# Layer 0 by seven block products, fewer PSUM banks for the sums, and a VectorE transpose for the row of scores

## The chip, the core and the metric

The kernel runs on one core of a Trainium2 chip. A core has five engines with a queue each: TensorE (PE) multiplies matrices into PSUM, VectorE (DVE) and ScalarE (ACT) do elementwise work, GpSimd (POOL) a few small operations, SyncE (SP) issues DMAs. Each queue is worked off in order, and engines wait for one another by semaphores. The metric is the device time of one launch in microseconds (us), the median of several runs.

## The reference

32 graphs, each with 512 nodes of 256 features and a 0/1 adjacency matrix, go through four attention layers. Every layer normalises the features, takes relu, and adds what the layer gives to x. Cut to what matters:

```python
h = maximum(layernorm(x), 0)
# layer 0: attention by a bilinear score, two rounds of convolution
q = h @ att_W;  score = q @ h.T / sqrt(256)
p = softmax(score + where(adj == 1, 0, -1000))
y = tanh(p @ (h @ W0 + b0));  x = x + tanh(p @ (y @ W1 + b1))
# layers 1, 2: score of an edge = a number of its row + a number of its column
Wh = h @ W.T                       # layer 2: h @ W
e = leaky_relu((Wh @ a1)[:, None] + (Wh @ a2)[None, :])
x = x + softmax(where(adj > 0, e, -9e15)) @ Wh       # layer 2: exp(-e), masked, divided by its row sum, elu
# layer 3: both kinds of score together, then two projections
f = h @ W;  logits = (f @ a_1).T + f @ a_2 + (f @ a_12) @ f.T
x = x + elu(h @ W_1 + (softmax(masked leaky_relu(logits)) @ h) @ W_2)
```

All products are in float32.

## The kernel before

A graph is worked in tiles of 128 nodes (NT = 4) and 128 features (HC = 2). `normed` computes the statistics on VectorE, a power on GpSimd, the scaled relu on ScalarE, then splits the float32 numbers into two 16-bit planes (VectorE), turns each by a DMA transpose, and joins them again (ScalarE, L488). The result is hT, features on partitions.

`attend` (L662) multiplies the transposed weights of the attention, tile by tile, by the values v, which carry a column of ones for the row sums. Layer 0 uses the same weights a second time (`again`, L723), and projects with W1 (L741).

Every step is recorded with `op(engine, cost, after, emit, ...)`: its engine, an assumed time (how long it holds the engine, and until when its result is there), the steps it waits for, and the buffers that it uses. `Plan.order` then puts the steps of all 32 graphs in an order, engine by engine, by these times and by a rank for each graph; at most FLIGHT = 5 graphs are under way. The instructions are emitted in this one order, and the framework adds the semaphore waits. So the order of each queue is fixed when the program is built, and can be read from it. Buffers of 4 KB a partition come from a pool of 36 pages; PSUM has 8 banks.

**Seven block products.** In layer 3 a product of two matrices, each cut into 2 x 2 blocks, is made from seven products of blocks in place of eight. `block_sums` forms four sums of blocks of a factor on VectorE (L570), `seven_of` does it once for a weight matrix, and `seven` runs the products:

```python
first = times(1, 0, True)                       # times(product, bank, fresh)
c11 = out(write, 0, 0, 0, first)
c12 = out(write, 0, 1, 0, times(6, 0, False, c11))
c22 = out(write, 1, 1, 0, times(7, 0, False, c12))
c21 = out(write, 1, 0, 0, times(4, 0, False, c22))
c11 = out(add, 0, 0, 1, times(2, 1, True, first), c11)
c22 = out(add, 1, 1, 2, times(5, 2, True, first), c22)
c12 = out(add, 0, 1, 2, times(3, 2, False, c22), c12)
```

Products 1, 6, 7, 4 add up in bank 0, which is written out after each; product 2 is in bank 1, products 5 and 3 in bank 2, and these are added to what was written. It is used for the features (L838, written by ScalarE L841, added by VectorE L846), the values (L855, L865, L868), the scores (L878, written by VectorE L885, added by L893) and the projection w (L855, L946, L950) of layer 3.

**Layer 0 without it.** `features_t` makes fa with att_sb (L513, copied by ScalarE L517), the values come from L682 (bias added by VectorE L686), the scores from L696, whose exponential ScalarE takes straight from PSUM (L700); VectorE applies the mask (L703).

**Row of scores in layers 1 and 2.** `scored_values` multiplies hT by weights with two more columns (L596); these give each node two numbers, which VectorE copies to `sd` (L600): the number of node 128 t + p lies at partition p, place t. `leaky_exp_t` needs the first number of all nodes as a row on every partition. In the first five and last five graphs TensorE turns it (L619); in the 22 others a DMA writes it to DRAM and a second one spreads it over the partitions (L624, L628), with the nodes in the order p, t. ScalarE then reads it with a step of 4 elements and applies the leaky relu (L635), and the exponential (L639).

**Weights.** ScalarE's queue issues the loads of w0, att and b0 first (L363 to L365), GpSimd's queue those of the other weights; the preparation of layers 1 to 3 runs on TensorE and VectorE beside graph 0.

Of the kernel before, what the change touches and what calls it, by code (L numbers as in the profile page):

```python
# [11 lines left out]
F32 = mybir.dt.float32  # L12
# [7 lines left out]
P = 128  # L20
# [22 lines left out]
V_SUM, V_INTO, V_BLOCK = (334.0, 425.0), (640.0, 730.0), (790.0, 880.0)  # L43
# [3 lines left out]
D_OUT, D_SPREAD = (550.0, 3500.0), (550.0, 4500.0)  # L47
# [111 lines left out]
def kernel(  # L159
# [37 lines left out]
    PAGES, VALUES = 36, 4  # L197
# [20 lines left out]
        "st": ([P, NT, 6], F32, None), "mv": ([P, NT, 2], F32, None), "sd": ([P, 2, NT], F32, None),  # L218
# [3 lines left out]
    POOLS = {"page": PAGES, "v": VALUES, "code": 1, "adj": 1, "planes": 3, "planesT": 2, "bank": 8,  # L222
# [129 lines left out]
    att_sb, w0_sb, w1_sb = (tile_of(n, H) for n in ("att_sb", "w0_sb", "w1_sb"))  # L352

    l3_w1s, m3 = (tile_of(n, HALF, 7) for n in ("l3_w1s", "m3"))
# [8 lines left out]
    nc.scalar.dma_start(out=w0_sb, in_=rows_of(w0))  # L363
    nc.scalar.dma_start(out=att_sb, in_=rows_of(att_w))
    nc.scalar.dma_start(out=b0_sb, in_=line_of(b0))  # L365
    ready["w1"] = [load(w1_sb, rows_of(w1))]
# [32 lines left out]
    for i in range(VALUES):  # L399
        v = const.tile([P, NT, LEAD + H + 1], F32, tag=f"v{i}", name=f"v{i}")  # L400
        nc.gpsimd.memset(v[:, :, LEAD + H :], 1.0)
        v_bufs.append(v)


    def graph(b, adj_before, x_before):
# [99 lines left out]
        def features_t(l, hs, w_sb, ready):  # L505

            done = []
            for k in range(HC):
                key = f"bank_f{l}{k}"

                def product(k, key):
                    for c in range(HC):
                        nc.tensor.matmul(T[key], w_sb[:, c, k * P : (k + 1) * P], T[f"hT{l}"][:, c, :],  # L513
                                         start=(c == 0), stop=(c == HC - 1))

                def evacuate(k, key):
                    nc.scalar.copy(T[f"fa{l}"][:, k, :], T[key])  # L517

                a = op("PE", pe(n512=4), hs + ready, partial(product, k, key), key, f"hT{l}")
                done.append(op("A", A_COPY, [a], partial(evacuate, k, key), key, f"fa{l}"))  # L520
            return done

        def seven(key, cost, after, keys, work, write, add):

            def times(x, k, fresh, *wait):
                name = f"bank_{key}{k}"
                return op("PE", cost, after(x) + list(wait), lambda: work(x, T[name], fresh), name, *keys)

            def out(how, i, l, k, *wait):
                return how(i, l, f"bank_{key}{k}", list(wait))


            first = times(1, 0, True)
            c11 = out(write, 0, 0, 0, first)
            c12 = out(write, 0, 1, 0, times(6, 0, False, c11))
            c22 = out(write, 1, 1, 0, times(7, 0, False, c12))
            c21 = out(write, 1, 0, 0, times(4, 0, False, c22))
            c11 = out(add, 0, 0, 1, times(2, 1, True, first), c11)  # L550
            c22 = out(add, 1, 1, 2, times(5, 2, True, first), c22)
            c12 = out(add, 0, 1, 2, times(3, 2, False, c22), c12)
            return {(0, 0): c11, (0, 1): c12, (1, 0): c21, (1, 1): c22}
# [31 lines left out]

        def scored_values(l, hs, w_aug, ready):
# [4 lines left out]
            for t in range(NT):  # L591
# [7 lines left out]
                def scores(t, key):  # L599
                    nc.vector.tensor_copy(T[f"sd{l}"][:, : cols - H, t], T[key][:, H:cols])  # L600
# [9 lines left out]
        def leaky_exp_t(l, ss, sign):  # L610

            turned = b < FLIGHT or b >= B - FLIGHT
# [3 lines left out]
            def turn(t):  # L618
                nc.tensor.transpose(T[key][:, t * P : (t + 1) * P],  # L619
                                    T[f"sd{l}"][:, 0, t : t + 1].to_broadcast([P, P]), ident)  # L620

            def collect():
                line.append(dram.tile([P, NT], F32, tag=f"row_{T.places['slot']['number']}", name=f"row{l}_{b}"))
                nc.sync.dma_start(out=line[0], in_=T[f"sd{l}"][:, 0, :])  # L624
# [5 lines left out]
            def leaky(c):  # L630
                if turned:
                    row = T[key].rearrange("q (t p) -> q t p", t=NT)
                else:
                    row = T[key][:, 0, :].rearrange("q (p t) -> q t p", t=NT)
                nc.scalar.activation(e(l, c).rearrange("q (t p) -> q t p", t=NT), row, AF.Prelu,  # L635
                                     bias=T[f"sd{l}"][:, 1, c : c + 1], alpha=ALPHA)
# [8 lines left out]
            else:  # L645
                a = op("D", D_OUT, ss, collect)
                a = op("D", D_SPREAD, [a], spread, key)
            ls = [op("A", A_PRELU, [a], partial(leaky, c), key, f"e{l}_{c // 2}") for c in range(NT)]
# [22 lines left out]

        hs = normed(0, [got_x] * NT)
        qs = features_t(0, hs, att_sb, [])
        vs = []
        for g in range(NT // 2):
            key = f"bank_v0{g}"

            def values(g, key):
                for j in range(2):
                    t = 2 * g + j  # L680
                    for c in range(HC):
                        nc.tensor.matmul(T[key][:, j * H : (j + 1) * H], T["hT0"][:, c, t * P : (t + 1) * P],  # L682
                                         w0_sb[:, c, :], start=(c == 0), stop=(c == HC - 1))

            def biased_v(g, j, key):
                nc.vector.tensor_add(T["v0"][:, 2 * g + j, LEAD : LEAD + H], T[key][:, j * H : (j + 1) * H], b0_sb)  # L686

            a = op("PE", pe(n256=8), hs[two(g)], partial(values, g, key), key, "hT0")
            vs += [op("V", V_ADD, [a], partial(biased_v, g, j, key), key, "v0") for j in range(2)]
        es = []  # L690
        for c in range(NT):
            key = f"bank_q{c}"

            def similar(c, key):
                for k in range(HC):
                    nc.tensor.matmul(T[key], T["hT0"][:, k, c * P : (c + 1) * P], T["fa0"][:, k, :],  # L696
                                     start=(k == 0), stop=(k == HC - 1))

            def exp0(c, key):
                nc.scalar.activation(e(0, c), T[key], AF.Exp, scale=float(H) ** -0.5)  # L700

            def masked0(c):
                nc.vector.tensor_tensor(e(0, c), e(0, c), T["mask0"][:, c, :], ALU.mult)  # L703

            a = op("PE", pe(n512=4), qs, partial(similar, c, key), key, "hT0", "fa0")
            a = op("A", A_COPY, [a], partial(exp0, c, key), key, f"e0_{c // 2}")
            es.append(op("V", V_MASK, [a, m0], partial(masked0, c), "mask0", f"e0_{c // 2}"))
# [128 lines left out]

# [21 lines left out]
        def two_tiles(key, k):  # L858
            return T[key][:, : 2 * k].rearrange("p (j k) -> p j k", j=2)
# [172 lines left out]
```

The softmax here doesn't subtract the row's maximum and nothing guards it: scores larger than these inputs give would overflow.

## Time and profile before

| | |
|---|---|
| median of 3 runs | 2461.58 us (2461.34 to 2461.85) |
| the profiled execution | 2461.46 us, its span from first to last instruction 2459.7 us |
| granted TensorE clock | 0.998 |
| TensorE matmul busy | 2407.4 us, 10700 records |
| TensorE weight loads busy | 1877.3 us |
| VectorE busy | 1876.2 us |
| ScalarE busy | 1742.8 us |
| time between the same step of two graphs in the middle | 75.3 us |

The profile is of one execution. Records of an engine can overlap: the end of one lies behind the start of the next, so the busy time of a row divided by its count is shorter than the mean duration where instructions follow each other closely. A float32 product appears as two matmul records. In rows of groups the columns are: line, engine, operation, output and inputs, shapes, count; then busy us and mean ns of one; then the idle time in front of it and what ended it. In rows of waits they are: who waited for whom, us in total, times, and the longest.

### The profile page before, as it was taken

Reading aid. Unit: us, or ns where it says so; the run is one execution under the profiler, and the core shown is the slowest. Engines: PE = TensorE matmul, PEld = TensorE weight load, DVE = VectorE, ACT = ScalarE, POOL = GpSimd, SP = SyncE. Lnnn points to the kernel's source line nnn. Section 1 sums busy time; section 2 is a strip of 40 time slices with the busy share of each in tenths; the row PEclk is TensorE's granted clock in tenths of the full one; section 3 lists DMA queues with packets and bytes.
Section 4 is the critical chain, followed back from the end, with each engine's and each line's share of the span. In section 5 each row is a group of like instructions: output and inputs, shape, how many; then the busy total and the mean of one; then the engine's idle time right before and its main releaser. Section 6 shows DMA issues by size and latency. Waiting matters only on the chain.

```text
span 2459.7 us, 33966 instructions
## 1 busy us (share of the span) xinstructions
PE 2407.4 (98%) x10700; PEld 1877.3 (76%) x10700; DVE 1876.2 (76%) x5733; ACT 1742.8 (71%) x3233; POOL 253.8 (10%) x315
## 2 busy tenths in 40 slices
PE   7999999999999999999999999999999999999998
PEld 4678777777777777777777777777777777777877
DVE  5468878777777877787777777777777778756888
ACT  4466777767777777777677777777776777755884
POOL 2001001110010101011101101010011011100110
PEclk9999999999999999999999999999999999999999
DMA  7223333332333322333323333233333343321221
GB/s 178 46 56 82 73 69 82 82 74 54 80 76 82 82 64 64 80 80 82 71 54 81 74 82 82 64 65 80 80 76 70 62 83 81 71 46 22 44 46 41
DMA packets 437204, 175.92 MB, mean 72 GB/s; under 512 B 393408, under 2 KB 410432, under 8 KB 437024
## 3 DMA queue, kind: packets, MB, share of 16 engines
q1 hardware_dynamic: 430976, 154.34, 29.9%
q0 software_dynamic: 5360, 18.75, 2.3%
q8 instruction: 85, 1.39, 0.2%
q14 instruction: 95, 0.78, 0.1%
q10 hardware_dynamic: 688, 0.66, 0.1%
HBM read 64.49 MB, written 16.87 MB: 33 GB/s over the span
## 4 chain that ended last, share of the span: by engine, by line
PE 73%; ACT 17%; DVE 5%; issue 3%; DMA 2%; POOL 0%; SPq 0%; POOLq 0%; ACTq 0%; DVEq 0%
PE bank_a L662 28%; PE bank_v L596 9%; PE bank_z L723 9%; ACT e L635 8%; PE bank_o L741 4%; PE bank_f L513 4%; PE bank_f L838 4%; PE bank_w L855 4%; ACT e L639 3%; PE bank_q L696 3%; PE bank_v L855 3%; PE bank_s L878 3%; ACT xn L475 2%; PE bank_v L682 2%; ACT e L700 1%
## 5 line engine op out<-in xcount | busy, mean ns | idle before, releaser
L662 PE MATMUL bank_a<-v,e 128*128 128x257 f32 (+1 forms) x4096 | 978.0, 381 | 21.8 <-ACT y L714 17.5
L662 PEld LDWEIGHTS bank_a<-v,e 128*128 128x128 f32 x4096 | 757.9, 190 | 199.9 <-issue 68.6
L488 ACT COPY hT<-planesT 128x512 uint16<-128x512 uint16 x512 | 383.2, 767 | 42.1 <-DMA planesT<-planes 41.7
L468 POOL TENSOR_TENSOR rstd<-ve,mhalf 128x2 f32<-128x2 f32 x256 | 215.2, 849 | 1891.7 <-DVE ve L465 1807.6
L475 ACT ACTIVATE xn<-x,off,rstd 128x256 f32<-128x256 f32 x512 | 277.3, 593 | 123.1 <-DVE off L471 119.3
L596 PE MATMUL bank_v<-l_aug,hT 128*128 128x258 f32 x1024 | 251.5, 383 | 3.3 <-ACT r L807 1.7
L480 DVE COPY planes<-xn 128x512 uint16<-128x512 uint16 x512 | 207.9, 422 | 43.8 <-ACT xn L475 24.1
L723 PE MATMUL bank_z<-e,y 128*128 128x512 f32 x512 | 240.6, 592 | 0.0
L696 PE MATMUL bank_q<-fa,hT 128*128 128x512 f32 x512 | 239.3, 592 | 0.0
L596 PEld LDWEIGHTS bank_v<-l_aug,hT 128*128 128x128 f32 x1024 | 192.2, 191 | 35.5 <-issue 3.6
L461 DVE BATCH_NORM_STATS2 st<-x 128x6 f32<-128x256 f32 x512 | 209.0, 408 | 6.6 <-DMA x<-in_x_dram 6.6
L635 ACT ACTIVATE e<-row,sd 128x512 f32<-128x512 f32 x176 | 207.0, 1229 | 0.0
L603 ACT COPY v<-bank_v 128x256 f32<-128x256 f32 x256 | 92.9, 375 | 90.1 <-PE bank_v L596 75.8
L639 ACT ACTIVATE e<-e 128x512 f32<-128x512 f32 x256 | 151.9, 632 | 0.0
L696 PEld LDWEIGHTS bank_q<-fa,hT 128*128 128x128 f32 x512 | 94.9, 190 | 71.4 <-issue 60.8
L723 PEld LDWEIGHTS bank_z<-e,y 128*128 128x128 f32 x512 | 96.5, 190 | 69.1 <-issue 57.9
L885 DVE SCALAR_TENSOR_TENSOR e<-bank_s,v,mask 128x256 f32<-128x256 f32 x256 | 111.1, 476 | 16.5 <-PE bank_s L878 16.3
L682 PE MATMUL bank_v<-w_sb,hT 128*128 128x256 f32 x512 | 121.4, 380 | 0.0
L703 DVE TENSOR_TENSOR e<-e,mask 128x512 f32<-128x512 f32 x128 | 87.5, 688 | 44.0 <-ACT e L700 43.9
L741 PE MATMUL bank_o<-w_sb,zT 128*128 128x256 f32 x512 | 120.4, 379 | 0.0
L513 PE MATMUL bank_f<-hT,att_sb 128*128 128x512 f32 x256 | 119.8, 593 | 0.0
L682 PEld LDWEIGHTS bank_v<-w_sb,hT 128*128 128x128 f32 x512 | 97.1, 191 | 23.9 <-issue 6.1
(134 smaller groups left out, 3702.1 us busy)
## 6 DMA issues: line engine op xcount, KB each, us to landing
adj<-in_adj_dram SPq DMA_DIRECT2D x128, 256.0 KB, 2.9
x<-in_x_dram SPq DMA_DIRECT2D x32, 512.0 KB, 5.1
out_dram<-y POOLq DMA_DIRECT2D x32, 512.0 KB, 4.1
row<-row SPq DMA_DIRECT2D x44, 256.0 KB, 3.7
planesT<-planes SPq DMA_TRANSPOSE x512, 2.4
codeT<-code SPq DMA_TRANSPOSE x128, 2.6
crest<-crest SPq DMA_TRANSPOSE x64, 2.4
raw_w<-in_L_gnn_W_dram POOLq DMA_DIRECT2D x3, 256.0 KB, 7.1
```

The lines of the kernel that those rows point to most:

```text
L468: nc.gpsimd.tensor_tensor(T[f"rstd{l}"][:, two(g)], T[f"ve{l}"][:, two(g)], mhalf[:, two(g)], ALU.pow)
L475: nc.scalar.activation(T[f"xn{l}"][:, t, :], T["x"][:, t, :], AF.Relu, bias=T[f"off{l}"][:, t : t + 1], scale=T[f"rstd{l}"][:, t : t + 1])
L488: nc.scalar.copy(bits[:, :, :, t * P : (t + 1) * P], T[f"planesT{l}_{t}"].rearrange("p (b c) n -> p b c n", b=2))
L513: nc.tensor.matmul(T[key], w_sb[:, c, k * P : (k + 1) * P], T[f"hT{l}"][:, c, :], start=(c == 0), stop=(c == HC - 1))
L596: nc.tensor.matmul(T[key][:, :cols], T[f"hT{l}"][:, c, t * P : (t + 1) * P], w_aug[:, c, :], start=(c == 0), stop=(c == HC - 1))
L635: nc.scalar.activation(e(l, c).rearrange("q (t p) -> q t p", t=NT), row, AF.Prelu, bias=T[f"sd{l}"][:, 1, c : c + 1], alpha=ALPHA)
L639: nc.scalar.activation(e(l, c), e(l, c), AF.Exp, scale=sign)
L662: nc.tensor.matmul(T[keys[j]][:, : LEAD + H + 1 - lead], e(l, c)[:, t * P : (t + 1) * P], T[f"v{l}"][:, c, lead:], start=(c == 0), stop=(c ...
L682: nc.tensor.matmul(T[key][:, j * H : (j + 1) * H], T["hT0"][:, c, t * P : (t + 1) * P], w0_sb[:, c, :], start=(c == 0), stop=(c == HC - 1))
L696: nc.tensor.matmul(T[key], T["hT0"][:, k, c * P : (c + 1) * P], T["fa0"][:, k, :], start=(k == 0), stop=(k == HC - 1))
L723: nc.tensor.matmul(T[f"bank_z{k}"], T["y0"][:, c, k * P : (k + 1) * P], e(0, c), start=(c == 0), stop=(c == NT - 1))
L741: nc.tensor.matmul(T[key][:, j * H : (j + 1) * H], T["zT"][:, k, t * P : (t + 1) * P], w1_sb[:, k, :], start=(k == 0), stop=(k == HC - 1))
```

## The change

It has four parts.

1. Layer 0's features, values and scores are made by `seven` as well. att and w0 are loaded into pages and cut into seven block matrices by VectorE (`seven_of`); sums hs0 of hT and fs0 of fa are formed for every graph. The values are written and added by VectorE, the features written by ScalarE and added by VectorE. Of the scores, three blocks are copied by ScalarE, get their addition from VectorE and then their exponential in SBUF; the fourth gets its exponential from PSUM.
2. `seven` holds one or two banks in place of three: products 2, 5 and 3 go to bank q, or (`beside`) to the second half of bank p. Features (layers 0 and 3), layer 0's values and w are of the second kind. Products 2 and 5 wait for more than before.
3. The two numbers of each node go to a buffer that is kept for a graph's slot and starts at zero: tile t's first number to column 32 t, its second to column 128 + t. In the middle graphs a VectorE transpose of 32 x 32 squares puts the first numbers on partitions 0, 32, 64 and 96; the DMA from there writes them in the order of the nodes, and the leaky relu reads a contiguous row.
4. Pages 35 for 36, and other assumed times for some steps.

```diff
-V_SUM, V_INTO, V_BLOCK = (334.0, 425.0), (640.0, 730.0), (790.0, 880.0)
+V_SUM, V_BLOCK = (334.0, 425.0), (790.0, 880.0)
+V_SQUARES = (180.0, 270.0)
-D_OUT, D_SPREAD = (550.0, 3500.0), (550.0, 4500.0)
+D_OUT, D_SPREAD = (550.0, 2500.0), (550.0, 4500.0)
...
-    nc.scalar.dma_start(out=w0_sb, in_=rows_of(w0))
-    nc.scalar.dma_start(out=att_sb, in_=rows_of(att_w))
+    w0_sb, att_sb = raw("raw9"), raw("raw10")
     nc.scalar.dma_start(out=b0_sb, in_=line_of(b0))
+    for n, dst, w, key in (("att", att_s, att_w, "raw10"), ("w0", w0_s, w0, "raw9")):
+        a = prepare("A", (500.0, 4000.0), [], lambda w=w, key=key: nc.scalar.dma_start(out=raw(key)(), in_=rows_of(w)), key)
+        ready[n] = seven_of(raw(key), dst, HALF, [a], key)
...
+    score_bufs = []
+    for i in range(FLIGHT):
+        s = const.tile([P, P + NT], F32, tag=f"scores{i}", name=f"scores{i}")
+        nc.gpsimd.memset(s, 0.0)
+        score_bufs.append(s)
...
+        def seven(key, cost, after, keys, work, write, add, beside=0):
+            p, q = f"bank_{key}p", f"bank_{key}{'p' if beside else 'q'}"
+            def times(x, bank, start, fresh, *wait):
+                return op("PE", cost, after(x) + list(wait), lambda: work(x, T[bank][:, start:], fresh), bank, *keys)
+            c11 = write(0, 0, p, 0, [times(1, p, 0, True)])
+            two = times(2, q, beside, not beside, c11)
+            c12 = write(0, 1, p, 0, [times(6, p, 0, False, c11)])
+            c22 = write(1, 1, p, 0, [times(7, p, 0, False, c12)])
+            four = times(4, p, 0, False, c22)
+            c21 = write(1, 0, p, 0, [four])
+            c11 = add(0, 0, q, beside, [two, c11])
+            c22 = add(1, 1, q, beside, [times(5, q, beside, True, four, c11), c22])
+            c12 = add(0, 1, q, beside, [times(3, q, beside, False, c22), c12])
...
-                    nc.vector.tensor_copy(T[f"sd{l}"][:, : cols - H, t], T[key][:, H:cols])
+                    nc.vector.tensor_copy(scores_of()[:, 32 * t : P + 1 + t : P - 31 * t], T[key][:, H:cols])
...
+            def squares():
+                nc.vector.transpose(T[f"sT{l}"], scores_of()[:, :P])
...
-                nc.sync.dma_start(out=line[0], in_=T[f"sd{l}"][:, 0, :])
+                nc.sync.dma_start(out=line[0].rearrange("(t g j) -> g t j", t=NT, j=32),
+                                  in_=T[f"sT{l}"][0:P:32, :].rearrange("g (t j) -> g t j", t=NT))
...
-                nc.scalar.activation(e(l, c).rearrange("q (t p) -> q t p", t=NT), row, AF.Prelu,
-                                     bias=T[f"sd{l}"][:, 1, c : c + 1], alpha=ALPHA)
+                row = T[key] if turned else T[key][:, 0, :]
+                nc.scalar.activation(e(l, c), row, AF.Prelu, bias=scores_of()[:, P + c : P + c + 1], alpha=ALPHA)
...
+        right_after, right = block_sums("hs0", "hT0", lambda j, l, T=T: T["hT0"][:, j, half(l)], hs, left=False)
+        qs = features_t(0, right_after, right, att_s, ready["att"])
...
+        vs = seven("v0", pe(nt=4), lambda x, after=right_after: after(x) + ready["w0"], ("hT0", "hs0"),
+                   partial(by_nodes, w0_s, right), write_v0, add_v0, beside=N // 2)
+        left_after, left = block_sums("fs0", "fa0", lambda i, j: T["fa0"][:, j, half(i)], qs, left=True)
...
+        def write_q(i, l, key, start, after):
+            if (i, l) == (1, 0):
+                return op("A", A_COPY, after, partial(exp0, i, l, key), key, f"e0_{l}")
+            return op("A", A_COPY, after, lambda: nc.scalar.copy(block_e0(i, l), two_tiles(key, 0, N // 2)), key, f"e0_{l}")
+        def add_q(i, l, key, start, after):
+            a = op("V", V_MASK, after, lambda: nc.vector.tensor_tensor(
+                block_e0(i, l), block_e0(i, l), two_tiles(key, 0, N // 2), ALU.add), key, f"e0_{l}")
+            exps.append(op("A", A_EXP, [a], partial(exp0, i, l), f"e0_{l}"))
+            return exps[-1]
...
+        qb = seven("q0", pe(n256=4), lambda x, right_after=right_after, left_after=left_after: right_after(x) + left_after(x),
+                   ("hT0", "hs0", "fa0", "fs0"), partial(scores0, right, left), write_q, add_q)
+        es = {il: op("V", V_MASK, [a, m0], partial(masked0, *il), "mask0", f"e0_{il[1]}") for il, a in qb.items()}
```

## The prediction

> **What bounds the kernel now.** I read the busy times first, then the stretches in which nothing starts or ends, then what TensorE waits for there, and last the groups of the lines that the change touches.
>
> ```profile
> PE 2407.4 (98%) x10700; PEld 1877.3 (76%) x10700; DVE 1876.2 (76%) x5733; ACT 1742.8 (71%) x3233; POOL 253.8 (10%) x315
> ...
> PE   7999999999999999999999999999999999999998
> ```
>
> TensorE is busy in every slice but the first and last. "Busy" can flatter it, since its records overlap, so I took the stretches, and 18 whole graphs (607.87 to 1963.95 us, 75.34 us each):
>
> ```profile
> 0.00:20.00 20.00, 4.98 (x22) 4.53 (x22) 8.25 (x33) 3.46 (x5) 12.26 (x30) 1.00 0.98 278
> ...
> 607.87:1963.95 1356.08, 1340.14 (x5941) 1045.58 (x5941) 1052.05 (x3205) 1000.84 (x1819) 139.03 (x162) 1.00 0.34 74
> ```
>
> The columns are length, then busy PE, PEld, DVE, ACT, POOL, then granted clock. In the middle PE lacks 0.89 us a graph; VectorE is busy 58.4 us and ScalarE 55.6 us of 75.34. Over the whole span PE is idle 52 us: about 16 in the first 40 us, 16 in the last 160, the rest in the middle. There the waits name one cause, once a graph:
>
> ```profile
> PE bank_a L662 <- ACT y L714: 15.7, 18, 0.9
> ```
>
> So the middle is bound by TensorE's stream, and what is saved there comes off the time if PE stays fed. The pace of the stream is read from starts, not from durations (each has 0.16 us of tail that overlaps):
>
> ```profile
> 1050.28 0.60 PE L855 MATMUL bank_w<-l_w1s,hT 128*128 128x128 f32 x4
> 1050.72 1.04 PE L662 MATMUL bank_a<-v,e 128*128 128x259 f32 x4
> ...
> 1000.74 1.88 PE L696 MATMUL bank_q<-fa,hT 128*128 128x512 f32 x4
> 1002.46 0.61 PE L855 MATMUL bank_v<-l_aug,hT 128*128 128x129 f32 x4
> ```
>
> Four records of 128 columns take 0.44 us (110 ns each), four of 512 columns 1.72 us (429 ns). An f32 product is two such records. Over the 18 graphs the mean from start to start is 111, 215.5 and 429 ns for 128, 256 and 512 columns.
>
> **The products of layer 0.** Features: 8 records of 512 (8 x 0.429 = 3.43 us) become 14 of 256 (3.02), -0.42. Values: 16 of 256 (3.45) become 28 of 128 (3.11), -0.34. Scores: 16 of 512 (6.86) become 28 of 256 (6.03), -0.83. Together -1.60 us a graph, x32 = **-51 us**, if the short records flow as now.
>
> A rule speaks against the values' part. The Trainium skill (TensorE: Matmul & The Clock Gate, "LDWEIGHTS (loading the stationary operand)") makes a weight load cost its columns over 1.2 GHz, 107 ns for 128 columns whatever the products behind it. Then a 128-column record is as short as its load, and if the two alternated, each would cost about 217 ns: 28 x 0.217 = 6.1 us in place of 3.45, +84 us over all graphs. The rows above show 110 ns with a new load before each record, so load and stream overlap; I use 111.
>
> **What VectorE gets.** Its rows are costed from start to start as well: a pair of L686 (0.42 us each) fills 0.75 us, so each holds VectorE 0.33.
>
> ```profile
> 1014.17 0.75 DVE L686 TENSOR_TENSOR v<-bank_v,b_sb 128x256 f32<-128x256 f32 x2
> ...
> L893 DVE TENSOR_TENSOR e<-e,bank_s 128x512 f32<-128x512 f32 x96 | 64.7, 681 | 3.0 <-PE bank_s L878 2.9
> ```
>
> Per graph: 8 block sums (hs0, fs0) x 0.33 = 2.7; 3 additions of features 1.0; values 7 in place of 4, +1.0; 3 additions of scores like L893, 0.60 each, 1.8; the masks stay 4. In the 22 graphs that spread by DMA, two 128x128 transposes: no row of before is one; the nearest, a 128x128 VectorE copy at the start, took 0.22 us, and 0.31 is the price in the Trainium skill (VectorE: DVE Perf Modes, "The three transpose paths", for bf16). I take 0.25, ends 0.2 and 0.6: 0.5 a graph. Sum +7.0: VectorE comes to 65.4 of some 74 us, **88%** instead of 78%. It is no bound, but it is now close enough that its queue answers late.
>
> **What ScalarE gets.** Features 4 copies at 0.32 for 2 at 0.53, +0.2; scores 3 copies and 3 more exponentials in place of 3, +1.7. Against that the row of scores lies in order, so L635 no longer reads every fourth element:
>
> ```profile
> L635 ACT ACTIVATE e<-row,sd 128x512 f32<-128x512 f32 x176 | 207.0, 1229 | 0.0
> ...
> L635 ACT ACTIVATE e<-bank_r,sd 128x512 f32<-128x512 f32 x80 | 52.4, 693 | 14.0 <-PE bank_r L619 13.9
> ```
>
> The contiguous form costs 0.69 to 0.72 (L924 reads SBUF, 716 ns): 8 x -0.52 = -4.2 us a graph in the middle. ScalarE ends at about 53 us a graph. I give this **0 us** of the time: ScalarE is off the path, five graphs overlap, and the work that hides it is TensorE's stream. If that cover were gone it would be worth 4 us a graph. The DMA pair behind it is hidden too (SP issues the same two DMAs a layer; the first now carries 16 runs of 128 B in place of 128 of 16 B); SP's queue gets nothing new.
>
> **What the banks cost.** This is the part that the trace of before cannot show. In layer 3 the first write chain had a bank of its own and the additions two others; ScalarE and VectorE never read the same bank. Now features of layers 0 and 3 and the w product hold all in one bank, written by ScalarE, added by VectorE. The Trainium skill (PSUM — Partial Sum Buffer, "PSUM bank collisions raise a hardware error") says that any two engines on one bank must be kept apart, readers too, at whatever columns. The built program's queues do so: in graph 16, the VectorE addition of product 2 stands behind product 4, ScalarE's write of product 4 waits for that addition, and product 5 waits for ScalarE. Counting from the start of product 4: result 0.60 (two records of 256, as L838), addition 0.42 (L846), copy 0.38 (L603), three hops of 0.05: 1.55 us. Between the two TensorE has product 4 itself (0.43) and one pair of 129-column products (0.44). It stands for **0.68 us**. By the rows alone, columns being disjoint, it would be nothing; by the program's waits I take them. Going so through the queues of graphs 16 and 17, I find one or two such places each, 0.5 to 0.7 us a graph; in the same stretch of before none. I take 0.5 x 32 = **+16 us**. Ends: 0 (VectorE and ScalarE ahead, other work in between) and 2 us a graph, +64 (all three chains catching).
>
> **The old stall.** L662 waiting for L714 is a wait for a bank to come free. Fewer banks are held now, and behind the tanh the new queue has 2.6 us of other products. But VectorE at 88% will be late elsewhere. From -0.87 x 22 = -19 to +30; I take **-6 us**.
>
> **The start.** Before, VectorE's first work is graph 0's statistics at 5.64 us; the weights of layer 0 are used as they land.
>
> ```profile
> 5.64 0.43 DVE L461 BATCH_NORM_STATS2 st<-x 128x6 f32<-128x256 f32 x1 [4.77 <-DMA x<-in_x_dram]
> ...
> 12.69 0.15 DVE L471 SCALAR_TENSOR_TENSOR off<-mv,rstd 128x2 f32<-128x2 f32 x1
> ```
>
> Now the seven block matrices of att and w0 stand ahead of those statistics in VectorE's queue, and ScalarE's queue issues b0, att, w0 in that order. Its last of the same 640 KB landed at 11.4 us (issue at 1.83, 9.6 to landing). Then 1.4 us of blocks, 2.2 of statistics, and power, code and copies as before: the offset of L471 comes at about 17.3, 4.6 later, and 16 us behind it TensorE's first features. Part is slack (TensorE did preparation from 26.3 to 28.9). The first f and q chains are also serial, where no other graph fills. I take **+6 us**, ends +2 and +12. **The end:** layer 3's additions come after product 4 now, about 1 us for each of its chains, partly filled by the second last graph: **+2**, ends 0 and 5.
>
> **Sum.** -51 + 16 - 6 + 6 + 2 = -33. The profiled execution took 2461.46 us (span 2459.7 and 1.8 around it), 0.1 under the median of 2461.58; so **2428 us**.
>
> **Rivals.**
> - The stream saving comes whole (0.18): the short distances are filled, because VectorE and ScalarE run ahead. -51 - 14 + 6 = 2402. For it: PE lacked only 0.89 us a graph so far. Against: VectorE's 10% more.
> - The banks eat most of it (0.17): all mixed chains catch, 1 to 1.5 us a graph, -51 + 32 to 48: 2443 to 2458. For it: the waits are in the program; against: in most places the queue has over 0.8 us between.
> - **Slower (0.07):** VectorE becomes the bound. It is an in-order queue, and each addition that now waits for a later product holds all behind it: block sums, masks and statistics of other graphs. It decides once these holds exceed 75.3 - 65.4 = 9.9 us a graph; twelve mixed-bank reads a graph at 0.9 us would do it. At 11 us a graph the period is 76.4, +35, with the start +6: about 2500; right at the point, 2468.
> - That the change does not do what it says is left out for the products: the queues hold 5876 products for 5396, 32768 columns fewer, as counted above.
>
> **How the numbers follow.** My case (2412 to 2443) 0.58, full saving 0.18, banks 0.17 (a quarter of that within 0.2% of before), slower 0.07 (2 of it within). 0.2%, 4.9 us, is about what a measurement of this kernel can tell from no change: 2456.7 to 2466.5. Faster 0.89, same 0.05, slower 0.06. The range leaves out the ends: 2402 to 2454.
>
> **What would show it.** Right: PE's stretch per middle graph near 73 us of stream; L855-like 128-column records of bank_v0 at 111 ns; waits of PE on bank_f, released by ACT fa, of 0.3 to 0.7 us once or twice a graph; VectorE 86 to 90% busy; the first features after 30 us; L635's successor near 0.7 us. Wrong: PE waits of over 2 us a graph, or VectorE busy over 95% in the middle (then slower); PE idle under 0.5 us a graph (then 2402); 128-column records at over 150 ns.

## The result, and the profile after

| | before | after |
|---|---|---|
| median | 2461.46 us (2460.83 to 2461.85, 4 runs) | 2425.9 us (2423.93 to 2429.52, 4 runs) |
| ratio to before on the same chip | | 0.9857, 95% interval 0.984 to 0.9875 |
| profiled execution, its span | 2461.46, 2459.7 us | 2423.93, 2422.2 us |
| one graph in the middle (output of graph to output of graph, mean of 18) | 75.32 us | 73.46 us |

The forecast of 2428 us was 2 us off. The experiments below show that errors cancel in this sum; how large they are depends on the order in which the parts are counted (see the last sums of the section on the prediction). First the page of after, its rows of busy time and TensorE's slices:

```profile
PE 2372.1 (98%) x11660; PEld 1988.7 (82%) x11660; DVE 2059.8 (85%) x6333; ACT 1727.2 (71%) x3393; POOL 252.0 (10%) x320
...
PE   6999999999999999999999999999999999999998
```

TensorE has 960 records more and 35.3 us less of busy time. VectorE rose by 184 us, ScalarE fell by 16. The same stretches as before, from the busy times of windows (length, then PE, PEld, DVE, ACT, POOL, clock):

```profile
0.00:20.00 20.00, 4.40 (x20) 4.02 (x20) 7.04 (x31) 1.67 (x2) 10.36 (x31) 1.00 0.66 201
...
607.87:1963.95 1356.08, 1350.21 (x6673) 1139.33 (x6672) 1183.96 (x3648) 1000.11 (x1961) 138.62 (x167) 1.00 0.35 77
```

VectorE is busy 87% of this stretch, where 88% was forecast. The short records flow as computed. From the timeline of PE (start, duration; four records are two products):

```profile
856.20 0.61 PE L702 MATMUL bank_v0p<-w_s,hs 128*128 128x128 f32 x4
856.64 1.03 PE L906 MATMUL bank_s3p<-hs,fa 128*128 128x256 f32 x4
857.51 1.03 PE L729 MATMUL bank_q0p<-fa,hs 128*128 128x256 f32 x4
```

From 856.20 to 856.64 four records of 128 columns pass, 110 ns each, each behind a new weight load. The Trainium skill (TensorE: Matmul & The Clock Gate, "LDWEIGHTS (loading the stationary operand)") has 107 ns for a load of 128 columns; the load records here last 191 ns, and still the products follow each other every 110 ns. Loads and products do not alternate, and the doubled price was rightly left out. The load records of layer 0's values, and the groups of the row of scores:

```profile
L702 PEld LDWEIGHTS bank_v0p<-w_s,hs 128*128 128x128 f32 x512 | 73.7, 191 | 7.9 <-DVE v L714 2.1
...
L632 ACT ACTIVATE e<-row,scores 128x512 f32<-128x512 f32 x176 | 117.6, 711 | 0.0
...
L619 DVE STREAM_TRANSPOSE sT<-scores 128x128 f32<-128x128 f32 x44 | 13.5, 306 | 0.3
```

The leaky relu takes 711 ns where it took 1229, and the transpose of squares 306. Of TensorE's waits, those of before for a bank that ScalarE's tanh holds (L714 there) are gone; in the middle this is left:

```profile
PE bank_f0p L676 <- ACT fa L684: 4.3, 9, 0.5
PE bank_v3p L702 <- ACT v L893: 0.3, 1, 0.3
```

This is the wait that the prediction worked out from the queues. One of them in the timeline of after:

```profile
839.77 0.59 PE L676 MATMUL bank_f0p<-hs,att_s 128*128 128x256 f32 x2
840.20 0.61 PE L702 MATMUL bank_v3p<-l_aug,hT 128*128 128x129 f32 x4
840.40 0.42 DVE L691 TENSOR_TENSOR fa<-fa,bank_f0p 128x256 f32<-128x256 f32 x1 [0.67 <-PE bank_f0p L676]
...
840.86 0.37 ACT L684 COPY fa<-bank_f0p 128x256 f32<-128x256 f32 x1 [0.85 <-DVE fa L691]
...
841.28 0.70 PE L676 MATMUL bank_f0p<-hs,att_s 128*128 128x256 f32 x2 [0.47 <-ACT fa L684]
```

Product 4 starts at 839.77, VectorE adds at 840.40, ScalarE copies at 840.86, product 5 starts at 841.28: 1.51 us, 1.55 were computed. TensorE had work until 840.20 + 4 x 0.11 = 840.64, so it stood 0.64 us (0.68 computed). The row says 0.47, because the last record before it ends 0.17 us after its place in the stream (840.81 for 840.64). A stall shorter than that tail shows as no idle time at all. Therefore I measure a **gap** from here on as the time from the start of a matmul record to the next start, less the pace of its shape (111, 217 or 429 ns), where that leaves over 25 ns. Stretches of a few us in which the profile's granted clock is halved are left out of the sums. Sums of such gaps in the profiled executions, split at the fifth and the 23rd output to leave:

| gaps, us | to the 5th output | 5th to 23rd | from there on | sum |
|---|---|---|---|---|
| before | 8.2 | 21.0, all L662 | 15.3 | 44.5 |
| after | 23.2 | 14.8, 12.7 of it bank_f0p | 14.2 | 52.2 |

After has more gaps than before. So of the 51 us of stream that the change saves, and the wait for the tanh that went, much was given back, and the question is which part of the change brought what.

### The profile page after: what moved, and what is told of

It reads as the page before. It is cut to its first block, busy times and chain, and to the rows that moved or that the text cites. A ratio compares the mean times of both kernels' runs of the same rounds, so it can differ in the third digit from the quotient of the medians.

```text
span 2422.2 us, 36547 instructions
## 1 busy us (share of the span) xinstructions
PE 2372.1 (98%) x11660; PEld 1988.7 (82%) x11660; DVE 2059.8 (85%) x6333; ACT 1727.2 (71%) x3393; POOL 252.0 (10%) x320
## 3 DMA queue, kind: packets, MB, share of 16 engines
q8 instruction: 92, 1.51, 0.3%
## 4 chain that ended last, share of the span: by engine, by line
PE 88%; ACT 4%; DVE 3%; issue 3%; DMA 1%; POOL 0%; ACTq 0%; POOLq 0%; DVEq 0%
PE bank_a L659 34%; PE bank_z L774 9%; PE bank_v L591 8%; PE bank_o L792 4%; PE bank_q0p L729 4%; PE bank_s3p L906 4%; PE bank_f0p L676 4%; PE bank_v0p L702 4%; PE bank_w3p L702 3%; PE bank_f3p L676 3%; PE bank_q0q L729 3%; PE bank_s3q L906 3%; PE bank_v3p L702 2%; PE bank_v3q L702 2%; ACT xn L484 1%
## 5 line engine op out<-in xcount | busy, mean ns | idle before, releaser
L659 PE MATMUL bank_a<-v,e 128*128 128x257 f32 (+1 forms) x4096 | 976.1, 381 | 7.9 <-ACT e L632 2.7
L659 PEld LDWEIGHTS bank_a<-v,e 128*128 128x128 f32 x4096 | 757.7, 190 | 158.9 <-issue 49.6
L635 ACT ACTIVATE e<-e 128x512 f32<-128x512 f32 x256 | 153.1, 626 | 0.0
L632 ACT ACTIVATE e<-row,scores 128x512 f32<-128x512 f32 x176 | 117.6, 711 | 0.0
L913 DVE SCALAR_TENSOR_TENSOR e<-bank_s3p,v,mask 128x256 f32<-128x256 f32 x256 | 111.2, 476 | 6.9 <-PE bank_s3p L906 6.8
L686 ACT ACTIVATE fa<-bank_f3p,l_u 128x256 f32<-128x256 f32 x128 | 60.6, 473 | 74.3 <-PE bank_f3p L676 71.9
L471 DVE BATCH_NORM_AGGREGATE mv<-st 128x2 f32<-128x6 f32 x512 | 93.2, 182 | 17.5
L792 PEld LDWEIGHTS bank_o<-w_sb,zT 128*128 128x128 f32 x512 | 96.4, 190 | 13.9 <-DVE st L470 0.2
L737 ACT ACTIVATE e<-e 128x512 f32<-128x512 f32 x96 | 60.6, 631 | 50.7 <-DVE e L746 50.0
L800 ACT ACTIVATE z<-z 128x512 f32<-128x512 f32 x64 | 40.2, 629 | 74.3 <-DVE z L796 74.2
```

The source lines that it names most:

```text
L659: nc.tensor.matmul(T[keys[j]][:, : LEAD + H + 1 - lead], e(l, c)[:, t * P : (t + 1) * P], T[f"v{l}"][:, c, lead:], start=(c == 0), stop=(c ...
L792: nc.tensor.matmul(T[key][:, j * H : (j + 1) * H], T["zT"][:, k, t * P : (t + 1) * P], w1_sb[:, k, :], start=(k == 0), stop=(k == HC - 1))
```

## Experiments

Times are medians of four runs; the ratio is to the kernel before on the same chip, which took 2463.3 to 2465.6 us beside these. Its 95% interval reaches some 0.15% to either side. "Period" is the time of a graph in the middle as above.

### The row of scores alone

The kernel before with part 3 of the change, and products, banks and weights as before:

```diff
+                nc.vector.transpose(T[f"sT{l}"], scores_of()[:, :P])
...
-                    row = T[key][:, 0, :].rearrange("q (p t) -> q t p", t=NT)
+                row = T[key] if turned else T[key][:, 0, :]
```

> The kernel before with the new way of the row of scores alone (VectorE transpose, ordered DMA, contiguous read by ScalarE); layer 0 by eight products, three banks a chain. Theory: ScalarE loses 90 us of work that was hidden; within 8 us of before, 2454 to 2462. Rival: in the old order ScalarE held banks (the wait of L662 for the tanh, 0.87 us a graph), and its relief takes that wait away: 2435 to 2450 us.

2439.1 us (2438.64 to 2439.43), ratio 0.9892 [0.9877, 0.9907], period 74.24. The part that I had costed at nothing brings 0.0108 x 2462 = 27 us when it is made alone, as much as three quarters of the whole gain. The waits of L662 for the tanh are gone, and gaps of TensorE fall from 44.5 to 18.0 us. This kernel has a new order of all queues, so the next one keeps the old order.

### ScalarE's read alone, in the order of before

```diff
-                    row = T[key][:, 0, :].rearrange("q (p t) -> q t p", t=NT)
+                    row = T[key][:, 0, :].rearrange("q (t p) -> q t p", t=NT)
```

> The kernel before in its own queue order and with its own DMAs; only ScalarE's leaky relu of the 22 middle graphs reads the row contiguously (the row is then permuted, so that part of the result differs). Theory (the tanh came late because the strided read holds ScalarE 0.5 us longer than the order assumes, 8 times a graph): ScalarE busy falls by 80 to 95 us, the wait of L662 for the tanh (15.7 us in the 18 middle graphs) falls below 3 us, period 74.2 to 74.6 for 75.32, time 2436 to 2446. Rival (row_only's gain came from its new order and shorter DMA times in the plan): the wait stays over 10 us, period 75.1 or more, time 2455 to 2466.

2439.99 us (2436.99 to 2442.23), ratio 0.9902 [0.9887, 0.9917], period 74.15. The theory holds: queues and DMAs are as before (the scores only reach the nodes in another order), and nothing but the duration of one ScalarE instruction has changed,

```profile
L635 ACT ACTIVATE e<-row,sd 128x512 f32<-128x512 f32 x176 | 116.8, 714 | 0.0
```

and the gaps of the middle go from 21.0 to 0.0 us. TensorE is busy without a break there:

```profile
607.87:1963.95 1356.08, 1356.08 (x6048) 1065.76 (x6047) 1078.10 (x3257) 952.65 (x1854) 134.26 (x165) 1.00 0.35 76
```

How a ScalarE at 71% came to hold TensorE is in the timeline of before, ahead of one of the waits (lines of DVE, ACT and TensorE's L662):

```profile
789.73 1.20 ACT L635 ACTIVATE e<-row,sd 128x512 f32<-128x512 f32 x1
790.79 6.66 PE L662 MATMUL bank_a<-v,e 128*128 128x257 f32 x30
790.84 0.61 ACT L639 ACTIVATE e<-e 128x512 f32<-128x512 f32 x1
...
791.49 0.69 DVE L764 TENSOR_TENSOR e<-e,mask 128x512 f32<-128x512 f32 x1 [1.25 <-ACT e L639]
...
795.88 0.69 DVE L902 TENSOR_TENSOR crest<-e 128x512 bf16<-128x512 f32 x1
...
796.60 1.33 ACT L924 ACTIVATE e<-e,zero 128x512 f32<-128x512 f32 x2 [0.47 <-DVE crest L902]
...
797.84 0.82 ACT L714 ACTIVATE y<-bank_a,rs 128x256 f32<-128x256 f32 x2
798.34 0.92 PE L662 MATMUL bank_a<-v,e 128*128 128x257 f32 x3 [0.89 <-ACT y L714]
```

The mask L764 waits 1.25 us for an exponential behind a strided L635. All of VectorE's queue is then late, L902 with it; ScalarE's L924 waits for L902, and the tanh that frees a PSUM bank stands behind L924 in ScalarE's queue. The lateness is handed from ScalarE to VectorE and back before it reaches TensorE. With the contiguous read the same L764 waits 0.22 us, the same tanh follows its reciprocal at once, and the products run on:

```profile
787.29 0.69 DVE L764 TENSOR_TENSOR e<-e,mask 128x512 f32<-128x512 f32 x1 [0.22 <-ACT e L639]
...
790.82 6.45 PE L662 MATMUL bank_a<-v,e 128*128 128x257 f32 x29
...
793.83 0.91 ACT L714 ACTIVATE y<-bank_a,rs 128x256 f32<-128x256 f32 x2
```

Of VectorE's waits in the middle of before, these show the first hop (us, times, longest):

```profile
DVE e L703 <- ACT e L700: 27.2, 19, 1.7
DVE e L764 <- ACT e L639: 23.4, 19, 1.6
DVE e L791 <- ACT e L639: 23.1, 18, 1.9
```

With the contiguous read these three are 10.0, 1.8 and 0.9 us, and VectorE's three largest waits in the middle are for TensorE:

```profile
DVE rs L711 <- PE bank_a L662: 45.1, 70, 1.6
DVE rs L799 <- PE bank_a L662: 33.6, 33, 1.7
DVE rs L774 <- PE bank_a L662: 23.4, 55, 1.3
```

### The strided read, its duration told to the order

Before assumes 0.57 us for the leaky relu (0.69 to its result), in all graphs. Was the wrong figure in the order the fault, or the longer work itself?

```diff
+A_STEP = (1115.0, 1229.0)
...
-            ls = [op("A", A_PRELU, [a], partial(leaky, c), key, f"e{l}_{c // 2}") for c in range(NT)]
+            ls = [op("A", A_PRELU if turned else A_STEP, [a], partial(leaky, c), key, f"e{l}_{c // 2}") for c in range(NT)]
```

> The kernel before with the strided read kept, and its real duration (1.12 held, 1.23 to result) in the order's assumptions for the middle graphs, for 0.57 and 0.69. Theory (an order made with a wrong duration, not lack of ScalarE): the new order has the tanh in time, the wait of L662 falls below 5 us in the middle, period 74.2 to 74.8, time 2436 to 2450. Rival (ScalarE's longer work itself costs it, wherever it stands): the wait or its like stays over 10 us, 2453 to 2468.

2453.42 us (2450.35 to 2454.84), ratio 0.9955 [0.9941, 0.997], period 74.73. The time, and a wait of over 10 us, are those of the rival; only the period lies in the theory's range. The tanh is in time, but another result of ScalarE is late in its place, the joined hT.

```profile
PE bank_v L597 <- ACT hT L489: 10.4, 10, 2.3
```

So this order regains about 11 us of the 24 to 27. Whether another one would regain more is not shown.

### The strided read in the changed kernel

After in its own order of queues, with the old access in the 22 middle graphs:

```diff
-                row = T[key] if turned else T[key][:, 0, :]
+                row, to = (T[key], e(l, c)) if turned else (T[key][:, 0, :].rearrange("q (p t) -> q t p", t=NT),
+                                                            e(l, c).rearrange("q (t p) -> q t p", t=NT))
```

> The changed kernel with every queue in the same order; only ScalarE's leaky relu in the 22 middle graphs reads the row with a step of four elements again, as before the change, so that the scores reach the nodes in another order (that part of the result differs from the reference). Theory of the prediction: 0.52 us more for each of 8 reads a graph, ScalarE from about 53 to 57 us of 73.4, hidden behind TensorE: within 5 us of the changed kernel (2426), ScalarE busy up by about 90 us. Rival: the contiguous row is part of the gain because ScalarE releases banks earlier: up to 4 us a graph, 2440 to 2515 us, with new waits of PE on ACT.

2434.41 us (2432.51 to 2437.35), ratio 0.9882 [0.9867, 0.9897], period 73.64. This lies between the two expectations: ScalarE's busy time is 76 us longer, the kernel 0.0025 x 2462 = 6 us, just over what the two intervals leave open. Its middle has one new gap a graph, at bank_q0p of layer 0's scores (18 gaps, 3.6 us). In this order the same 0.52 us per instruction is worth about a quarter of what it was worth in before's.

### VectorE's 88%: the sums formed twice

Each of the 16 block sums of a graph is computed twice, which adds 16 x 0.33 = 5.3 us of VectorE a graph (an estimate from starts). The first kernel has the order of after; in the second the doubled time is told to the order:

```diff
                 nc.vector.tensor_tensor(d(x), first, second, how)
+                nc.vector.tensor_tensor(d(x), first, second, how)
...
-            one = op("V", V_SUM, after, partial(form, 1)
+            one = op("V", V_SUM2, after, partial(form, 1)
```

(The second part only in the second kernel, with V_SUM2 = (668, 759) for V_SUM = (334, 425), and likewise for the other sums.)

> The changed kernel with the same order of steps; each of the 16 block sums a graph (hs and fs of layers 0 and 3) is formed twice in a row by VectorE, 16 x 0.33 = 5.3 us a graph more, for which the order makes no room. Theory: VectorE goes from about 64 to 69 of 73.4 us a graph and is still no bound; TensorE's waits on DVE rise by some tenths of a us a graph: 2430 to 2450 us. Rival (VectorE is already the bound in stretches, its in-order queue passes every delay on): most of the 5.3 us a graph comes through, 2530 us or more.

> The changed kernel with each of the 16 block sums a graph formed twice, but now with the doubled time told to the planner, which orders all anew. In the unchanged order the same work cost 130 us, 4.1 us a middle graph. Theory A (the order, not VectorE's capacity, was short: VectorE needs 61 + 5.3 = 66 us of start-to-start time in a period of 73.5): most of it is hidden again, a period of 74 to 75 us, 2430 to 2475 us. Theory B (VectorE in an in-order queue is in effect the bound at 88% busy): a period of 77 us or more, 2540 us or more.

In after's order, as its rival had it: 2555.73 us (2554.41 to 2557.16), ratio 1.0373 [1.0358, 1.0389], period 77.57. 4.1 of the 5.3 us come through in each graph, with VectorE busy only 88% of the span. TensorE now waits for VectorE's additions (row of waits in the middle of this kernel):

```profile
PE bank_v3q L703 <- DVE v L897: 19.2, 17, 1.2
PE bank_f3p L677 <- DVE fa L692: 12.5, 9, 1.4
PE bank_w3p L703 <- DVE w L979: 11.7, 18, 1.2
```

Told to the order, the same work costs 2483.89 us (2482.63 to 2489.81), ratio 1.0081 [1.0064, 1.0098], period 74.32: 0.9 us a graph, at 91%. The period is that of its theory A, the time lies above A's range, because much of the loss came at the ends: the fifth output leaves at 566.7 us (545.4 in after), and from the 23rd to the last output it takes 571.7 us (549.6). So the share of busy time, 88% with a loss of 4.1 us a graph and 91% with one of 0.9, says little of VectorE's slack in this kernel. Its slack is what the order has left it at each place.

### The banks

First the old three-bank form of `seven` for every chain, layer 0's too; products 2, 5 and 3 then wait for no addition:

```diff
-            p, q = f"bank_{key}p", f"bank_{key}{'p' if beside else 'q'}"
...
+                name = f"bank_{key}{'pqs'[k]}"
...
+            c11 = out(add, 0, 0, 1, times(2, 1, True, first), c11)
+            c22 = out(add, 1, 1, 2, times(5, 2, True, first), c22)
```

> The changed kernel with the old seven of three banks a chain, for layer 3 and for layer 0's features, values and scores; ordered anew. Theory: no mixed bank any more, but seven chains a graph want 3 of 8 banks each; the attention's products wait for banks: 0.3 to 1 us a graph more than the changed kernel, 2433 to 2460 us. Rival: the planner fits them, the mixed-bank waits are gone, 2415 to 2425 us.

2422.99 us (2421.52 to 2423.83), ratio 0.9826 [0.9811, 0.9841], period 72.95, within the rival's range. The middle is 0.51 us a graph faster than in after, and bank_f0p's gaps there (12.7 / 18 = 0.7 a graph) are gone: gaps of 14.8 become 6.0, nearly all at bank_v of layers 1 and 2. But the first graphs are later: the fifth output leaves at 561.6 us (545.4 in after), so only a part of it reaches the total. Some 4 of these 16 us come with the granted clock. It is 0.50 there in two stretches of 6.8 us; one of them, as a window and in TensorE's timeline:

```profile
161.40:168.20 6.80, 5.55 (x13) 4.45 (x14) 2.12 (x4) 3.08 (x6) 0.00 (x0) 0.50 0.44 114
...
164.52 3.63 PE L659 MATMUL bank_a<-v,e 128*128 128x257 f32 x8
167.95 1.15 PE L729 MATMUL bank_q0p<-fs,hs 128*128 128x256 f32 x4
```

Eight records of 257 columns take 3.43 us, 429 ns each for the usual 217. The two stretches cost 5 us; after has one of 3.4 us before its fifth output, which costs 1.5. What sets them off is not shown.

Then two banks for the chains that share one, the waits of the chain kept:

```diff
-                         beside=N // 2)
+                         )
...
-partial(by_nodes, l3_w1s, right), write_w, add_w, beside=N // 2)
+partial(by_nodes, l3_w1s, right), write_w, add_w)
```

(The first edit is in `features_t`.)

> The changed kernel with a second bank for products 2, 5 and 3 of the features (layers 0 and 3) and of w, so that ScalarE and VectorE never read one bank of a chain; ordered anew. Theory: the waits of PE on bank_f0p released by ACT fa (0.5 us in every second middle graph) go, 0.2 to 0.5 us a graph or 6 to 15 us, less what fewer free banks cost: 2415 to 2424 us. Rival: the banks that are held longer bring back a wait for a free bank at the attention's products of 0.5 to 1 us a graph: 2430 to 2445 us.

2439.39 us (2438.46 to 2445.43), ratio 0.9909 [0.9893, 0.9926], period 73.60: slower than after. The gaps of layer 0's features are gone from the middle (12.7 us in after). In their place stand 10.1 us at layer 0's values, which still hold one bank, and 7.9 at bank_v of layers 1 and 2. Most of the loss comes before the fifth output (563.1 us), where a features chain of layer 3 stands once for 7.8 us (rows of TensorE's waits, whole run):

```profile
PE bank_f3p L676 <- ACT fa L686: 7.8, 1, 7.8
...
PE bank_v0p L701 <- DVE v L713: 6.2, 20, 0.3
```

The time is that of the rival, but the rival's wait, at the attention's products, is not what the middle shows. The granted clock has a part in it too: it was 0.992 to 0.996 in the four runs (0.998 to 0.999 in after), and its stretches at 0.50 hold 8 us in the profiled run, 1.5 in after's. Whether the shared bank costs, or the chain write, add, write that the code keeps here, the two kernels do not settle, since in each all queues were ordered anew.

### The values of layer 0 by eight products

After, with features and scores by seven, and the values as in before (L682 there); w0 is not cut:

```diff
-        vs = seven("v0", pe(nt=4), lambda x, after=right_after: after(x) + ready["w0"], ("hT0", "hs0"),
-                   partial(by_nodes, w0_s, right), write_v0, add_v0, beside=N // 2)
+            a = op("PE", pe(n256=8), hs[two(g)] + ready["w0"], partial(values, g, key), key, "hT0")
+            vs += [op("V", V_ADD, [a], partial(biased_v, g, j, key), key, "v0") for j in range(2)]
```

> The changed kernel with layer 0's values made by eight block products again (16 records of 256 columns a graph in place of 28 of 128; 4 VectorE additions in place of 7), w0 loaded once and not cut; ordered anew. Theory: the stream gets 0.34 us a graph longer, +11 us, against which VectorE's queue and the start get lighter by 1 us a graph and 4 us at the start: 2425 to 2437 us. Rival: the 128-column records and the additions cost more than the stream saves, and it is faster than the changed kernel: 2410 to 2422 us.

**2410.85 us** (2409.27 to 2411.39), ratio 0.9776 [0.9762, 0.9791], period 73.29: the best version of all, as its rival had it and 0.0081 x 2462 = 20 us better than after by the ratios (13 us by the two profiled executions), though its stream is 0.34 x 32 = 11 us longer. Its gaps in the middle are 3.7 us for 14.8, in all 30.2 for 52.2:

```profile
PE bank_v L592 <- ACT hT L498: 1.3, 2, 0.9
PE bank_f3p L677 <- DVE y L1006: 0.7, 1, 0.7
```

12 of its 13 us at the last output are gained from the 23rd output on (537.9 us for 549.6). This suggests that the seven products of the values were worth less than the chain that they brought. It does not show it: this kernel has a new order, and a new order alone was worth 13 us (start_late, below).

With the values so, the three banks for the other chains:

```diff
-            p, q = f"bank_{key}p", f"bank_{key}{'p' if beside else 'q'}"
...
+                name = f"bank_{key}{'pqs'[k]}"
```

> values_eight with the three-bank form of the seven products for every chain. Theory (shared banks still cost the features and w chains): TensorE's excess over its pace falls from 30 us by 5 to 15: 2398 to 2407. Rival (more banks held, so other products wait for a free bank): 2411 to 2422.

2415.51 us (2414.55 to 2416.52), ratio 0.9803 [0.9789, 0.9818], in the rival's range. The period is 73.14, but gaps rise from 30.2 to 35.1 us and the stretch from the 23rd output to the last takes 547.0 for 537.9. Whether a missing bank is the cause, as the rival says, was not traced.

### The start

The loads of att and w0 are assumed to take 9 and 13 us for 4, b0 is issued last; so VectorE's order puts the statistics of graph 0 ahead of the blocks.

```diff
-        a = prepare("A", (500.0, 4000.0), [], lambda w=w, key=key: nc.scalar.dma_start(out=raw(key)(), in_=rows_of(w)), key)
+        a = prepare("A", (500.0, 9000.0 if n == "att" else 13000.0), [], lambda w=w, key=key: ...
```

> The changed kernel with the assumed arrival of att and w0 later (9 and 13 us in place of 4), and b0 issued behind them, so that the first statistics stand ahead of the block matrices in VectorE's queue; the planner orders all else anew. Theory: the wait for these weights put off the first graph by 7 us; its features start near 29 us in place of 35.2, and 5 to 8 us come off: 2417 to 2422 us. Rival: the first 60 us are bound by DMA and by the chain of one graph anyway; no change within 3 us.

2416.08 us (2414.14 to 2416.36), ratio 0.9805 [0.979, 0.9819], 13 us better than after by the ratios (0.0052 x 2462), but not for the reason given. Its windows:

```profile
20.00:62.00 42.00, 33.76 (x172) 28.94 (x173) 33.94 (x117) 19.53 (x38) 2.90 (x4) 1.00 0.54 131
607.87:1963.95 1356.08, 1355.74 (x6717) 1150.02 (x6716) 1192.49 (x3674) 1005.45 (x1977) 135.55 (x168) 1.00 0.33 77
```

The first features start at 31.39 for 35.18 us, yet TensorE has done less by 62 us than in after (4.39 + 33.76 = 38.15 for 40.08). The gain came in the middle, where the new order has a period of 72.88 and gaps of 5.1 us in 18 graphs for 14.8 (all at bank_f0p, each under 0.2 us; idle time shows only 0.3 of it). Two assumed times and the place of b0's load, all of the start, have thus reordered the queues of all graphs, for the better by chance. The same with the values by eight:

```diff
-        a = prepare("A", (500.0, 4000.0), [], lambda w=w, key=key: nc.scalar.dma_start(out=raw(key)(), in_=rows_of(w)), key)
+        a = prepare("A", (500.0, 9000.0), [], lambda w=w, key=key: nc.scalar.dma_start(out=raw(key)(), in_=rows_of(w)), key)
```

> values_eight with the arrival times of start_late (att 9 us, w0 13 us, b0 issued last). Theory (each gain was its own): the start order is worth 3 to 10 us on top of values_eight: 2401 to 2408. Rival (start_late's gain was a chance of the new order in the middle, not repeated here): 2408 to 2420, middle period as in values_eight or longer (73.2 to 73.6).

2412.05 us (2409.53 to 2413.15), ratio 0.9786 [0.9769, 0.9802], period 73.28, as values_eight within the spread: it brings nothing there, as the rival had it. Against start_late the values by eight are 0.0019 x 2462 = 5 us ahead, less than the intervals tell apart.

## Why the prediction was right in sum, and wrong in two of its steps

- **Stream, -51: held.** 110 ns for a record of 128 columns. The saving of 1.6 us a graph shows best against before_contig, whose middle has no gaps: its records of 18 graphs take 1334.4 us at that pace, those of after 1307.5, 1.5 us a graph less.
- **ScalarE's contiguous row, 0, and the old stall, -6: the steps that failed.** Together they were worth 24 us (before_contig) to 27 us (row_only). The prediction knew the 4.2 us a graph and the wait for the tanh, and did not connect them: "ScalarE is off the path" was read from its 71%, while the wait of 0.87 us a graph was with ScalarE by name. The cover named, TensorE's stream, is no cover for a result that frees a bank for TensorE. What spoke against it in the trace was VectorE's list of waits, with ScalarE's exponentials in it, and the time assumed for L635, 0.57, beside the measured 1.12 from start to start. The -6 rested on fewer banks being held; before_contig holds as many as before and has no such wait. In the order of after the row is worth 6 us (row_strided), so the 24 belong to before's order.
- **Banks, +16: right in place, too small.** Place, chain and length of the stall (0.64 for 0.68 us) were as computed. But gaps in the middle are 14.8 / 18 = 0.8 us a graph, where 0.5 was taken: 54 gaps at bank_f0p, 27 of which are 103 ns and so cannot be seen in the profile's idle time, while 9 are 0.63 us like the one above. For 32 graphs it is 26 us, an estimate from the middle.
- **Start, +6: probably too small.** The forecast of the offset copy was 17.3 us:

```profile
9.87 0.29 DVE L343 COPY att_s<-raw_w 128x256 f32<-128x256 f32 x1 [8.99 <-DMA raw_w<-in_L_gnn_att_W_dram]
...
14.11 0.30 DVE L343 COPY w_s<-raw_w 128x256 f32<-128x256 f32 x1 [2.88 <-DMA raw_w<-in_L_gnn_W_dram]
...
15.38 0.42 DVE L470 BATCH_NORM_STATS2 st<-x 128x6 f32<-128x256 f32 x1
...
19.45 0.13 DVE L480 SCALAR_TENSOR_TENSOR off<-mv,rstd 128x2 f32<-128x2 f32 x1
```

  It came at 19.45: w0 landed at 14.1 in place of 11.4, and the statistics stood behind it as said. First features at 35.18 for 28.89 us. Up to the fifth output after has 15.0 us more gaps than before_contig (23.2 to 8.2), of which bank_f0p has 5 and L659 4: start and banks together, which these figures do not part.
- **End, +2: held.** Gaps behind the 23rd output are 2.0 us more than in before_contig (14.2 to 12.2).
- **VectorE at 88%, "no bound": right as it stands, too calm.** In sums_twice 4.1 of 5.3 us more a graph came through in this order. The rival's point, from which VectorE was to decide, 9.9 us of holds a graph, was far too late.

The sum: in medians, before_contig to after is (0.9857 - 0.9902) x 2462 = -11 us, so about 40 of the 51 us were lost, and 24 were forecast (16 + 6 + 2). Gaps and ends of the profiled executions explain 33 (spans 2440.4 to 2422.2, -18.2 = -51.2 + 31.8 of gaps + 1.2 outside of them); the other 7 are between runs and chips, as the profiled before_contig is the slowest of its four and the profiled after the fastest of its own. Against 16 us too little there stand 18 us too little for the row (24 for 6): counted so, the total of 2428 was right by these two. Counted with the row last, in the order of after, the rest of the change is worth (1 - 0.9882) x 2462 = 29 us, where 33 were forecast, and the row 6, where 0 was: the same two signs, but errors of 4 and 6 us. That the total came within 2 us was luck in either count.

## What to carry to other kernels

An engine's share of busy time does not say that it is off the path: look at whom the one remaining wait names, and follow that engine's queue back, through other engines too, to the instruction whose duration differs from what the order assumes. Measure TensorE's stalls by starts, not by idle time, and weigh a saved product against the waits that its form adds: here the kernel was fastest with one of three conversions left out. Where all queues are ordered anew by a planner, the order alone can move the time (13 us in start_late), so keep the order fixed in an experiment that is to show a cause.

## What the runs showed of the hardware that was not expected

- ScalarE reads a float32 row from SBUF with a step of 4 elements in 1229 to 1234 ns, contiguous in 711 to 714 ns (128x512, before and row_strided, after and before_contig).
- A VectorE transpose of 32 x 32 squares on 128x128 float32 took 306 ns, where 250 was taken. The 0.31 us of the Trainium skill (VectorE: DVE Perf Modes, "The three transpose paths"), given for bf16, was the better figure.
- In stretches of 3.4 to 6.8 us at a granted clock of 0.50 TensorE's records take twice as long: 429 ns for 257 columns where 217 is usual (three_banks). They cost 1.5 us in after's profiled run and 8 in mixed_apart's.
- A DMA of 256 KB that is third in ScalarE's queue, issued at 1.68 us, was waited for until 14.11 us; in before the last of the three, of 128 KB and issued at 1.83 us, took 9.6 us to land.
